# Graph convolutions by slots on one NeuronCore: 13 slots per pair, six gathered chunks per tile, blocks of nine tiles, tables kept in SBUF

## The chip, the cores and the metric

The kernel runs on one NeuronCore of a Trainium2 chip. The time is the device time of one execution in microseconds (us). The time before is the median of three runs. Beside these there is one profiled execution, from which all views, lines and durations come; it took longer than the unprofiled runs, and both are given below. The engines are PE (TensorE), DVE (VectorE), ACT (ScalarE), POOL (GpSimd) and SP (SyncE, which here issues the plain DMAs). Lines such as L1168 are lines of the kernel before.

## The reference

There are 12500 nodes with 128 features and 200000 edges, sorted by destination. Two layers with a residual are computed:

```python
h = relu(layernorm(x));  x = x + attention(h, edges, edge_attr)   # 8 heads, softmax over a node's incoming edges
h = relu(layernorm(x));  x = x + gcn(h)
# gcn: three times   h = conv(h, W, b);  relu after the first two;  h = batch_norm(h)
# conv: h = h @ W;  out[d] = sum over edges (s, d) and the loop (d, d) of h[s] * dinv[s] * dinv[d];  out + b
```

The widths are 128 -> 256 -> 128 -> 128. The norm dinv depends on a node's degree alone. The kernel scales the rows by dinv beforehand and the sums by dinv afterwards, so that a convolution is a plain sum of source rows for each destination.

## The kernel before

**Stages.** The prologue makes q, k and v. Attention runs over 106 tiles of TN = 118 destination nodes. Then place_edges (L681 to L817) sorts each tile's edges on DVE and writes tables. Then follow three convolutions, each with a dense transform behind it (L1211). The function fast (L661) holds all but the prologue. A second branch, conv_rows, is built in too, for edge lists that do not fit the slots; it does not run on this input.

**How a convolution sums.** The rows of the table are grouped by NS = 98 source blocks of 128 rows, all held in SBUF as hs. Each pair (tile, source block) has SB = 16 slots. An edge that finds a slot is served without a gather; what is left over goes to an overflow list of OV = 512 entries per tile, that is JO = 4 chunks of 128.

- `take(b)` (L1131) builds the slots of block b, TB = 8 tiles, so that 8 x 16 = 128 slots of one source block form a matrix. It loads the slot numbers gi (one byte each, the same for all partitions, L1136). DVE compares them with the partition number and so makes a selection matrix go (L1141), four source blocks at a time. PE multiplies it with hs (L1144), ACT copies the product from PSUM to stage (L1146), and after SG = 14 source blocks SP stores stage to m in DRAM (L1147). A block takes seven such groups, 98 products.
- `reduce(b)` (L1150) handles the 8 tiles of a block. For each tile POOL gathers the overflow rows from the table in DRAM (L1159, recorded at L150, the line of the helper gather), one indirect DMA per chunk. SP loads the tile's slots back from m as mr, 112 partitions of RC = 14 rows (L1162). DVE makes one-hot matrices oh from the destinations of slots (dsA, L1165) and of overflow (odA, L1166); both are recorded at L676, the line of one_hot. PE sums into zp: the tile's own rows tg (L1079), 14 products with mr (L1168) and 4 with the gathered rows (L1170).
- `finish` (L1070) is called for NG = 4 tiles at a time. It loads tg and the norms db, and after the products scales zp (L1082) and hands it on: to a product with W1 in the first convolution (L1241), else to a bias and ReLU on ACT; then come the statistics (L1185).

**What sets the order.** All loops are unrolled at build time. The kernel writes take(b) and then reduce(b - 2) (LEAD = 2, L1175). A scheduler orders each engine's instructions once, when the program is built, by the order in which they are written and by an estimate of when their inputs and buffers are free; on the chip each engine and each DMA queue then runs its list in order. Buffers: m 4 blocks, gi 2, go 3, stage 2, mr 3, rows 5 tiles, oh 2, and two PSUM banks each for gp, zp and hq.

**Tables.** place_edges stores four tables in DRAM: gi_d for take, ds_d for the slots' destinations, os_d and od_d for the overflow's sources and destinations. At its start, conv_slots loads dsA, osA and odA from them (L1119 to L1121), in runs of 56 or 16 bytes, in each of the three convolutions.

Of the kernel before, what the change touches and what calls it, by code (L numbers as in the profile page):

```python
# [37 lines left out]
SB = 16  # L38
OV = 512
JO = OV // P  # L40
TB = P // SB
SG = 14
RP = 112
# [5 lines left out]
def tile_gnn(ctx: ExitStack, tc: tile.TileContext, x, src, dst, ea, wqkvT, weT, w1, w2, w3, par, out):  # L49
# [20 lines left out]
    assert NS % SG == 0 and SL % RP == 0 and SL <= WE and NS * P * P < LATE and TN < P  # L70
    RC = SL // RP
# [20 lines left out]

    gi_d = dram.tile([NBK, NS, TB, SB], U8, name="gi_d")
    ds_d = dram.tile([NTT, SL], FP, name="ds_d")
    os_d = dram.tile([NTT, OV], I32, name="os_d")
    od_d = dram.tile([NTT, OV], FP, name="od_d")
# [563 lines left out]
    def fast():  # L660
# [3 lines left out]
        slotted = fc.tile([1, 1], I32, name="slotted")  # L664
        pars = fc.tile([P, 12], FP, name="pars")
# [13 lines left out]
        def place_edges(rt, ps):  # L679
# [8 lines left out]
            turn = 0  # L688

# [69 lines left out]
            xo = rt.tile([NTT, 2, OV], I32, name="xo")  # L759
            yo = rt.tile([NTT, OV], FP, name="yo")  # L760
            nc.vector.tensor_scalar(x[:, :OV], x[:, :OV], -1.0, None, op0=ALU.add)
            nc.vector.tensor_copy(xo[:, 0], x[:, :OV])
            nc.vector.tensor_scalar(xo[:, 1], xo[:, 0], P - 1, None, op0=ALU.bitwise_and)
            nc.vector.tensor_copy(yo, xo[:, 1])
            nc.sync.dma_start(od_d, yo)
            nc.vector.tensor_scalar(y[:, :OV], x[:, :OV], 0.0, None, op0=ALU.max)
            nc.vector.tensor_copy(xo[:, 0], y[:, :OV])
            nc.vector.tensor_scalar(xo[:, 0], xo[:, 0], 7, None, op0=ALU.logical_shift_right)
            nc.sync.dma_start(os_d, xo[:, 0])
# [35 lines left out]
            nc.sync.dma_start(ds_d, A[turn][:, :SL])  # L805
# [3 lines left out]
            for b in range(NBK):  # L809
                tn = min(TB, NTT - b * TB)  # L810
                nc.sync.dma_start(gi_d[b, :, :tn, :].rearrange("s t k -> t s k"),
                                  sl[b * TB:b * TB + tn, :].rearrange("t (s k) -> t s k", k=SB))
            if NTT % TB:
                none = rt.tile([NS, (TB - NTT % TB) * SB], U8, name="none")
                nc.vector.memset(none, 255)
                nc.sync.dma_start(gi_d[NBK - 1, :, NTT % TB:, :].rearrange("s t k -> s (t k)"), none)
# [252 lines left out]
        NST = -(-NTT // NG)  # L1069

        def finish(wk, table, t0, n, zp, use, ps, add):

            tg = wk.tile([TN, NG, D], FP, name="tg")
            nc.sync.dma_start(tg[:, :n, :], rows118(table, t0, n))
            db = wk.tile([P, NG * TN], FP, name="db")
            nc.sync.dma_start(db[:, :n * TN],
                              dinv_d[t0 * TN:(t0 + n) * TN].unsqueeze(0).to_broadcast([P, n * TN]))
            for i in range(n):
                nc.tensor.matmul(zp[:, i, :], tg[:, i, :], ident[:TN, :TN], start=True, stop=False)  # L1079
                add(i)  # L1080
            zt = wk.tile([P, NG * TN], FP, name="zt")
            nc.vector.tensor_tensor(zt[:, :n * TN], zp[:, :n].rearrange("p a b -> p (a b)"), db[:, :n * TN],  # L1082
                                    op=ALU.mult)
            use(wk, t0, n, zt[:, :n * TN], ps)

        def conv_rows(table, use):

            with ExitStack() as s:
                ew = s.enter_context(tc.tile_pool(name="ew", bufs=1))
                srcA = ew.tile([P, NTT, JJ], I32, name="srcA")  # L1090
                dlA = ew.tile([P, NTT, JJ], BF, name="dlA")
                nc.sync.dma_start(srcA, sw_d.rearrange("t (p j) -> p t j", j=JJ))
                nc.sync.dma_start(dlA, dlb_d.rearrange("t (p j) -> p t j", j=JJ))
                ga = s.enter_context(tc.tile_pool(name="ga", bufs=3))
                wk = s.enter_context(tc.tile_pool(name="wk", bufs=2))
                ps = s.enter_context(tc.tile_pool(name="ps", bufs=2, space=PSUM))
                for t0, n in groups(NTT, NG):
                    zp = ps.tile([P, NG, TN], FP, name="zp")

                    def add(i):  # L1100
                        rows = ga.tile([P, JJ, D], FP, name="rows")
                        for j in range(JJ):
                            gather(rows[:, j, :], table, srcA[:, t0 + i, j:j + 1])
                        oh = wk.tile([P, JJ, TN], FP, name="oh")
                        one_hot(oh, dlA[:, t0 + i, :])
                        for j in range(JJ):
                            nc.tensor.matmul(zp[:, i, :], rows[:, j, :], oh[:, j, :], start=False, stop=(j == JJ - 1))

                    finish(wk, table, t0, n, zp, use, ps, add)

        def conv_slots(table, use):


            with ExitStack() as s:
                tb = s.enter_context(tc.tile_pool(name="tb", bufs=1))
                dsA = tb.tile([RP, NTT, RC], FP, name="dsA")
                osA = tb.tile([P, NTT, JO], I32, name="osA")
                odA = tb.tile([P, NTT, JO], FP, name="odA")
                nc.sync.dma_start(dsA, ds_d.rearrange("t (p c) -> p t c", c=RC))  # L1119
                nc.sync.dma_start(osA, os_d.rearrange("t (p c) -> p t c", c=JO))  # L1120
                nc.sync.dma_start(odA, od_d.rearrange("t (p c) -> p t c", c=JO))  # L1121
                blocks = s.enter_context(tc.tile_pool(name="blocks", bufs=4, space=DRAM))
                gy = s.enter_context(tc.tile_pool(name="gy", bufs=2))
# [5 lines left out]
                ps = s.enter_context(tc.tile_pool(name="ps", bufs=2, space=PSUM))  # L1129

                def take(b):  # L1131
                    m = blocks.tile([TB * SB, NS, D], FP, name="m")
                    for s0 in range(0, NS, SG):
                        stage = sg.tile([P, SG, D], FP, name="stage")
                        gi = gy.tile([P, SG, P], U8, name="gi")
                        nc.sync.dma_start(gi.rearrange("p s m -> p (s m)"),  # L1136
                                          gi_d[b, s0:s0 + SG].rearrange("s t k -> (s t k)").unsqueeze(0)
                                          .to_broadcast([P, SG * P]))
                        for a, n in groups(SG, 4):
                            go = gx.tile([P, 4, P], FP, name="go")  # L1140
                            nc.vector.tensor_scalar(go[:, :n], gi[:, a:a + n], iota_q, None, op0=ALU.is_equal)  # L1141
                            gp = ps.tile([P, 4, D], FP, name="gp")
                            for i in range(n):
                                nc.tensor.matmul(gp[:, i, :], go[:, i, :], hs[:, s0 + a + i, :], start=True,  # L1144
                                                 stop=True)
                            nc.scalar.copy(stage[:, a:a + n, :], gp[:, :n, :])  # L1146
                        nc.sync.dma_start(m[:, s0:s0 + SG, :], stage)  # L1147
                    return m

                def reduce(b, m):  # L1150
                    for t0 in range(b * TB, min(NTT, (b + 1) * TB), NG):
                        n = min(NG, NTT - t0)
                        zp = ps.tile([P, NG, TN], FP, name="zp")

                        def add(i):
                            t = t0 + i
                            rows = ga.tile([P, JO, D], FP, name="rows")
                            for j in range(JO):
                                gather(rows[:, j, :], table, osA[:, t, j:j + 1])  # L1159
                            k = (t - b * TB) * SB  # L1160
                            mr = mt.tile([RP, RC, D], FP, name="mr")
                            nc.sync.dma_start(mr, m[k:k + SB].rearrange("k s d -> (k s) d")  # L1162
                                              .rearrange("(p c) d -> p c d", c=RC))
                            oh = wk.tile([P, RC + JO, TN], FP, name="oh")
                            one_hot(oh[:RP, :RC, :], dsA[:, t, :])  # L1165
                            one_hot(oh[:, RC:, :], odA[:, t, :])  # L1166
                            for j in range(RC):
                                nc.tensor.matmul(zp[:, i, :], mr[:, j, :], oh[:RP, j, :], start=False, stop=False)  # L1168
# [4 lines left out]
                        finish(wk, table, t0, n, zp, use, ps, add)  # L1173

                LEAD = 2  # L1175
                taken = []
                for b in range(NBK + LEAD):
                    if b < NBK:
                        taken.append(take(b))
                    if b >= LEAD:  # L1180
                        reduce(b - LEAD, taken[b - LEAD])

        def stats(st, h, t0, n):
            w = min(n * TN, N - t0 * TN)
            nc.vector.bn_stats(st[:, t0 // NG, :], h[:, :w])  # L1185
# [44 lines left out]
        def convolutions(conv):  # L1230
            with ExitStack() as s:
# [4 lines left out]
                def use1(wk, t0, n, zt, ps):  # L1236
                    a, b = t0 * TN, (t0 + n) * TN
                    hx = wk.tile([P, NG * TN], FP, name="hx")
                    for k, h in enumerate((big[:, a:b], hx[:, :b - a])):
                        hq = ps.tile([P, NG * TN], FP, name="hq")  # L1240
# [119 lines left out]
```

## Time and profile before

| | |
|---|---|
| median of 3 runs | 6388.98 us (6387.02 to 6391.8) |
| profiled execution, own time | 6587.43 us |
| its span, first to last instruction | 6585.6 us |
| busy: PE, DVE, POOL, ACT | 71%, 55%, 56%, 16% |
| DMA | 1134.9 MB in all; queue of SP 43.6% and of POOL 19.0% of 16 engines' span |
| HBM read, written | 797 MB, 332 MB |
| first to last gather of attention | 149 to 2801 us |
| first to last product of the convolutions | 3323.2 to 4369.4, 4461.5 to 5457.9, 5533.6 to 6525.9 us |

The page of the profile has the busy tenths of each engine in 40 equal slices of the span, with the granted clock of PE (PEclk) and the share of the DMA engines in use. Its groups are read so: line, engine, operation, what is written and read (partitions x elements), count | busy us, mean ns of one | idle us of the engine just before them, and what ended most of it. In the timeline a row gives start and length in us, engine, line and operation, how many instructions are merged, and in brackets the idle time before it with what ended it. SPq is the issue of a DMA by SP. PEld, the weight load, runs beside PE.

### The profile page before, as it was taken

The numbers are of one execution on the slowest core, as the hardware profiler recorded it, in microseconds if no ns is written. First come the engines' busy times: TensorE is split into PE (matmuls) and PEld (weight loads), VectorE is DVE, ScalarE is ACT, GpSimd is POOL, SyncE is SP. The second block draws the span as 40 slices with busy tenths as digits, with TensorE's granted clock in tenths as the row PEclk, the third lists the DMA queues.
The fourth block names the chain that finished last, engine by engine and source line by source line (L and its number), as shares of the span: only waits on it lengthen the run. The fifth ranks groups of instructions, "written<-read, shape, count | busy, mean of one in ns | idle before, by whom it ended". The sixth has DMA issues, their size and how long they took to land. (4 is left out here: it accounts for less than half of the span.)

```text
span 6585.6 us, 84666 instructions
## 1 busy us (share of the span) xinstructions
PE 4653.7 (71%) x30954; PEld 4338.3 (66%) x30954; DVE 3616.5 (55%) x6389; ACT 1073.6 (16%) x2501; POOL 3713.3 (56%) x2981
## 2 busy tenths in 40 slices
PE   5576776676666667710068888877888886888887
PEld 2566666666666666600068878877888886888887
DVE  7455655566565666699534444453444444444445
ACT  3111111111111111100022222202221212221220
POOL 1677777777777777700025555543556662556654
PEclk9677776777776777755588999998899998999988
DMA  6455555454454455400388888878788887888877
GB/s 181 131 134 130 137 133 131 127 126 127 117 128 124 124 132 129 112 5 3 42 211 238 232 243 243 234 191 225 242 244 246 246 233 183 245 249 240 241 230 205
DMA packets 710647, 1134.91 MB, mean 172 GB/s; under 512 B 299663, under 2 KB 528207, under 8 KB 710119
## 3 DMA queue, kind: packets, MB, share of 16 engines
q1 hardware_dynamic: 587581, 821.13, 43.6%
q0 software_dynamic: 122256, 306.67, 19.0%
q8 instruction: 251, 4.11, 0.3%
q10 hardware_dynamic: 388, 1.60, 0.1%
q14 instruction: 171, 1.40, 0.1%
HBM read 797.28 MB, written 331.80 MB: 171 GB/s over the span
## 5 line engine op out<-in xcount | busy, mean ns | idle before, releaser
L150 POOL DMA_INDIRECT rows<-t_d,osA x1272 | 1687.6, 1327 | 2034.8 <-PE zp L1079 773.6
L150 POOL DMA_INDIRECT kv<-kv_d,srcA x1696 | 2021.4, 1192 | 635.2 <-issue 491.7
L1144 PE MATMUL gp<-hs,go 128*128 128x128 f32 x8232 | 1134.8, 297 | 563.9 <-DMA rows<-t_d,osA 235.1
L1144 PEld LDWEIGHTS gp<-hs,go 128*128 128x128 f32 x8232 | 1060.7, 207 | 615.8 <-issue 480.5
L1168 PE MATMUL zp<-oh,mr 112*128 112x118 f32 x8904 | 1174.4, 290 | 133.6 <-DMA mr<-m 115.5
L1168 PEld LDWEIGHTS zp<-oh,mr 112*128 112x128 f32 x8904 | 1129.0, 206 | 148.5 <-issue 74.1
L945 PE MATMUL qe<-qt,oht 128*128 128x128 f32 x3392 | 869.1, 417 | 455.4 <-issue 192.6
L945 PEld LDWEIGHTS qe<-qt,oht 128*128 128x128 f32 x3392 | 775.0, 310 | 522.2 <-issue 368.2
L1141 DVE TENSOR_SCALAR go<-gi,iota_q 128x512 f32<-128x512 uint8 (+1 forms) x1176 | 512.8, 455 | 906.0 <-PE gp L1144 489.6
L676 DVE TENSOR_TENSOR oh<-iota_f,dsA 112x1652 f32<-112x1652 f32 x318 | 598.9, 1884 | 689.7 <-PE zp L1170 331.6
L1146 ACT COPY stage<-gp 128x512 f32<-128x512 f32 (+1 forms) x1176 | 599.4, 534 | 1736.5 <-PE gp L1144 1348.2
L946 DVE TENSOR_TENSOR kv<-qe,kv 128x512 f32<-128x512 f32 x424 | 289.0, 683 | 840.4 <-DMA kv<-kv_d,srcA 677.1
L1011 PE MATMUL acc<-vals,oh 128*118 128x137 f32 x3392 | 526.0, 323 | 110.5 <-DVE vals L1005 73.4
L1011 PEld LDWEIGHTS acc<-vals,oh 128*118 128x118 f32 x3392 | 504.9, 219 | 132.3 <-DVE vals L1005 91.3
L1170 PE MATMUL zp<-oh,rows 128*128 128x118 f32 x2544 | 343.7, 277 | 16.4 <-DMA rows<-t_d,osA 14.7
L1170 PEld LDWEIGHTS zp<-oh,rows 128*128 128x128 f32 x2544 | 314.8, 193 | 20.0 <-DMA rows<-t_d,osA 17.5
L1005 DVE TENSOR_TENSOR vals<-kv,vals 128x2048 f32<-128x2048 f32 x106 | 242.3, 2286 | 34.6 <-ACT vals L1004 13.1
L676 DVE TENSOR_TENSOR oh<-iota_f,dlA 128x1888 f32<-128x1888 f32 x106 | 224.4, 2117 | 61.4 <-remote 58.0
L961 PE MATMUL sm<-wbd,et 128*128 128x32 f32 x848 | 172.5, 362 | 115.6 <-DVE mg L998 92.4
L961 PEld LDWEIGHTS sm<-wbd,et 128*128 128x128 f32 x848 | 166.6, 292 | 124.8 <-DVE mg L998 99.5
L949 DVE TENSOR_REDUCE sc<-kv 128x128 f32<-128x2048 f32 x106 | 240.5, 2269 | 0.0
L676 DVE TENSOR_TENSOR oh<-iota_f,odA 128x472 f32<-128x472 f32 x318 | 203.6, 641 | 11.4 <-DMA odA<-od_d 11.4
(235 smaller groups left out, 3490.2 us busy)
## 6 DMA issues: line engine op xcount, KB each, us to landing
m<-stage SPq DMA_DIRECT2D x294, 896.0 KB
mr<-m SPq DMA_DIRECT2D x318, 784.0 KB
gi<-gi_d SPq DMA_DIRECT2D x294, 224.0 KB
dw_b<-dlb_d SPq DMA_DIRECT2D x106, 512.0 KB
kv<-kv_d,srcA POOLq DMA_INDIRECT x1696
ebx<-in_edge_attr_dram SPq DMA_DIRECT2D x106, 256.0 KB
rows<-t_d,osA POOLq DMA_INDIRECT x1272
tg<-t_d SPq DMA_DIRECT2D x78, 236.0 KB
```

The lines of the kernel that those rows point to most:

```text
L150: nc.gpsimd.indirect_dma_start(out=o, out_offset=None, in_=table[:, :], in_offset=bass.IndirectOffsetOnAxis(ap=idx, axis=0))
L676: nc.vector.tensor_tensor(oh, iota_f[:sh[0], :TN].unsqueeze(1).to_broadcast(sh), dl.unsqueeze(2).to_broadcast(sh), op=ALU.is_equal)
L945: nc.tensor.matmul(qe[:, k, :], ohv[:, :, j + k], qt, start=True, stop=True)
L946: nc.vector.tensor_tensor(qk[:, j:j + 4, :], qe, qk[:, j:j + 4, :], op=ALU.mult)
L961: nc.tensor.matmul(bias[:, 4 * k:4 * k + 4, :].rearrange("p j h -> p (j h)"), et[:, k, :], wbd, start=True, stop=True)
L1005: nc.vector.tensor_tensor(vh[:, :, :, :C], kv[:, :, D:].rearrange("p j (h c) -> p j h c", h=H), vh[:, :, :, C:].to_broadcast([P, JJ, H, C] ...
L1011: nc.tensor.matmul(acc, oh[:, j, :], va[:, j, :], start=(j == 0), stop=(j == JJ - 1))
L1141: nc.vector.tensor_scalar(go[:, :n], gi[:, a:a + n], iota_q, None, op0=ALU.is_equal)
L1144: nc.tensor.matmul(gp[:, i, :], go[:, i, :], hs[:, s0 + a + i, :], start=True, stop=True)
L1146: nc.scalar.copy(stage[:, a:a + n, :], gp[:, :n, :])
L1168: nc.tensor.matmul(zp[:, i, :], mr[:, j, :], oh[:RP, j, :], start=False, stop=False)
L1170: nc.tensor.matmul(zp[:, i, :], rows[:, j, :], oh[:, RC + j, :], start=False, stop=(j == JO - 1))
```

## The change

1. Slots and overflow: SB goes from 16 to 13, OV from 512 to 768, so that a tile has 1274 slots and six gathered chunks. A block has TB = 9 tiles (117 slots of a source block), and there are 12 blocks for 14.
2. A tile's slots are loaded as 127 partitions of RC = 10 rows and one of 4, in three DMAs; m is stored as 112 and 5 partitions, tg loaded as 112 and 6. gi has the tile outside and the slot inside, and go reads it permuted.
3. The order: one block is taken while the one before is reduced, and the tiles of the latter are written between the groups of the former. finish becomes a generator that yields after each tile. Groups of finish have GN = 3 tiles.
4. The tables dlS (destinations, bfloat16) and srcO (overflow's sources) stay in SBUF; the new helper turned fills them, with PE transposes. ds_d, os_d and od_d and their loads are gone. gi_d is stored in runs of 182 bytes.
5. The one-hot matrices of a tile are made by one instruction, from numbers that lie in PSUM (nums) and from dlS.

```diff
-SB = 16
-OV = 512
+SB = 13
+OV = 768
+GN = 3
...
+    RC = -(-SL // P)
+    LP, LR = divmod(SL, RC)
...
+        dlS = fc.tile([P, NTT, RC + JO], BF, name="dlS")
+        srcO = fc.tile([P, NTT, JO], I32, name="srcO")
...
+            def turned(a, n, o, copy):
+                av = a[:, :n * P].rearrange("t (p c) -> t c p", c=n)
+                for c, m in groups(n, 4):
+                    tp = ps.tile([P, 4, P], FP, name="et_p")
+                    for i in range(m):
+                        nc.tensor.transpose(tp[:, i, :NTT], av[:, c + i, :], ident[:NTT, :NTT])
+                    copy(o[:, :, c:c + m].rearrange("p t c -> p c t"), tp[:, :m, :NTT])
...
-            nc.sync.dma_start(od_d, yo)
+            turned(x1, JO, dlS[:, :, RC:], nc.scalar.copy)
...
-            nc.sync.dma_start(os_d, xo[:, 0])
+            turned(y1, JO, srcO, nc.vector.tensor_copy)
...
-            nc.sync.dma_start(ds_d, A[turn][:, :SL])
+            turned(A[turn], RC, dlS[:, :, :RC], nc.scalar.copy)
...
-                nc.sync.dma_start(gi_d[b, :, :tn, :].rearrange("s t k -> t s k"),
-                                  sl[b * TB:b * TB + tn, :].rearrange("t (s k) -> t s k", k=SB))
+                nc.sync.dma_start(gi_d[b, :, :tn, :].rearrange("g t k -> t g k"),
+                                  sl[b * TB:b * TB + tn, :].rearrange("t (g k) -> t g k", g=NS // SG))
...
-            nc.sync.dma_start(tg[:, :n, :], rows118(table, t0, n))
+            for a, b in ((0, 112), (112, TN)):
+                nc.sync.dma_start(tg[a:b, :n, :], rows118(table, t0, n, a, b))
...
                 nc.tensor.matmul(zp[:, i, :], tg[:, i, :], ident[:TN, :TN], start=True, stop=False)
                 add(i)
+                yield
...
-                nc.sync.dma_start(dsA, ds_d.rearrange("t (p c) -> p t c", c=RC))
-                nc.sync.dma_start(osA, os_d.rearrange("t (p c) -> p t c", c=JO))
-                nc.sync.dma_start(odA, od_d.rearrange("t (p c) -> p t c", c=JO))
-                blocks = s.enter_context(tc.tile_pool(name="blocks", bufs=4, space=DRAM))
-                gy = s.enter_context(tc.tile_pool(name="gy", bufs=2))
+                tb = s.enter_context(tc.tile_pool(name="tb", bufs=1, space=PSUM))
+                nums = tb.tile([P, TN], FP, name="nums")
+                nc.vector.tensor_copy(nums, iota_f[:, :TN])
+                blocks = s.enter_context(tc.tile_pool(name="blocks", bufs=3, space=DRAM))
+                gy = s.enter_context(tc.tile_pool(name="gy", bufs=3))
...
+                        gv = gi.rearrange("p t (s k) -> p s t k", k=SB)
                         for a, n in groups(SG, 4):
-                            nc.vector.tensor_scalar(go[:, :n], gi[:, a:a + n], iota_q, None, op0=ALU.is_equal)
+                            nc.vector.tensor_scalar(go[:, :n], gv[:, a:a + n], iota_q, None, op0=ALU.is_equal)
...
-                        nc.sync.dma_start(m[:, s0:s0 + SG, :], stage)
-                    return m
+                        for x, y in ((0, 112), (112, TS)):
+                            nc.sync.dma_start(m[x:y, g * SG:(g + 1) * SG, :], stage[x:y])
+                        yield
...
-                            nc.sync.dma_start(mr, m[k:k + SB].rearrange("k s d -> (k s) d")
-                                              .rearrange("(p c) d -> p c d", c=RC))
+                            for x, y, r in ((0, 112, RC), (112, LP, RC), (LP, LP + 1, LR)):
+                                nc.sync.dma_start(mr[x:y, :r], mv[x * RC:(y - 1) * RC + r]
+                                                  .rearrange("(p c) d -> p c d", c=r))
...
-                            one_hot(oh[:RP, :RC, :], dsA[:, t, :])
-                            one_hot(oh[:, RC:, :], odA[:, t, :])
+                            nc.vector.tensor_tensor(oh, nums.unsqueeze(1).to_broadcast(sh),
+                                                    dlS[:, t, :].unsqueeze(2).to_broadcast(sh), op=ALU.is_equal)
...
-                LEAD = 2
-                taken = []
-                for b in range(NBK + LEAD):
-                    if b < NBK:
-                        taken.append(take(b))
-                    if b >= LEAD:
-                        reduce(b - LEAD, taken[b - LEAD])
+                taken = None
+                for b in range(NBK + 1):
+                    tiles = reduce(b - 1, taken) if b else iter(())
+                    if b < NBK:
+                        taken = blocks.tile([TS, NS, D], FP, name="m")
+                        done = 0
+                        for g, _ in enumerate(take(b, taken)):
+                            while done < g * TB * SG // (NS - SG):
+                                next(tiles, None)
+                                done += 1
+                    for _ in tiles:
+                        pass
```

## The prediction

> **What bounds the kernel now.** I read the page first (slices, then groups), then one row per convolution from the busy times by stretch, then the timeline of a block and of the seams between convolutions. From the page, rows 2:
>
> ```profile
> POOL 1677777777777777700025555543556662556654
> PEclk9677776777776777755588999998899998999988
> DMA  6455555454454455400388888878788887888877
> ```
>
> Slices 1 to 17 (149 to 2801 us) are attention, 17 to 20 the placing of edges on DVE, 21 to 40 three convolutions. The change works on the last two only. The groups that matter there:
>
> ```profile
> L150 POOL DMA_INDIRECT rows<-t_d,osA x1272 | 1687.6, 1327 | 2034.8 <-PE zp L1079 773.6
> L1144 PE MATMUL gp<-hs,go 128*128 128x128 f32 x8232 | 1134.8, 297 | 563.9 <-DMA rows<-t_d,osA 235.1
> L1168 PE MATMUL zp<-oh,mr 112*128 112x118 f32 x8904 | 1174.4, 290 | 133.6 <-DMA mr<-m 115.5
> L1170 PE MATMUL zp<-oh,rows 128*128 128x118 f32 x2544 | 343.7, 277 | 16.4 <-DMA rows<-t_d,osA 14.7
> L676 DVE TENSOR_TENSOR oh<-iota_f,dsA 112x1652 f32<-112x1652 f32 x318 | 598.9, 1884 | 689.7 <-PE zp L1170 331.6
> ```
>
> Each product is two records: 8232 = 3 x 14 blocks x 98 slots x 2. By stretch, first to last product of each convolution:
>
> ```profile
> core 0: us, PE busy (x) PEld busy (x) DVE busy (x) ACT busy (x) POOL busy (x), PEclk, DMA share, GB/s
> 3323.20:4369.40 1046.20, 893.03 (x6880) 850.33 (x6880) 469.32 (x680) 233.56 (x446) 554.03 (x419) 0.92 0.80 235
> 4461.50:5457.90 996.40, 858.88 (x6768) 837.84 (x6768) 454.99 (x656) 216.66 (x418) 554.66 (x417) 0.91 0.80 239
> 5533.60:6525.90 992.30, 846.74 (x6712) 825.41 (x6712) 447.59 (x643) 213.10 (x410) 557.46 (x414) 0.92 0.79 237
> ```
>
> PE is the busiest at 86%, DMA is at 80%, and POOL waits for PE (773.6 us). The rest of PE's time is lost where a block turns from building slots to reducing and back:
>
> ```profile
> 4800.22 0.94 POOL L150 DMA_INDIRECT rows<-t_d,osA  x1 [0.30 <-issue]
> 4800.90 0.65 DVE L1082 TENSOR_TENSOR zt<-zp,db 128x472 f32<-128x472 f32 x1 [1.80 <-PE zp L1170]
> ...
> 4809.39 1.88 DVE L676 TENSOR_TENSOR oh<-iota_f,dsA 112x1652 f32<-112x1652 f32 x1 [1.03 <-PE zp L1170]
> 4809.48 3.16 POOL L150 DMA_INDIRECT rows<-t_d,osA  x1 [0.30 <-issue]
> 4811.19 0.64 DVE L676 TENSOR_TENSOR oh<-iota_f,odA 128x472 f32<-128x472 f32 x1
> 4812.76 4.98 PE L1168 MATMUL zp<-oh,mr 112*128 112x118 f32 x28 [3.19 <-DMA mr<-m]
> 4818.70 3.29 PE L1168 MATMUL zp<-oh,mr 112*128 112x118 f32 x28
> ```
>
> Two things to see. PE waits 3.19 us for a transfer and then does 14 products in 4.98 us that take 3.29 warm. And a gather takes 0.94 us beside a DVE operation that reads PSUM (zp), but 3.16 us when DVE builds a one-hot from two SBUF operands: it ends 0.8 us after DVE does. The seam before the second convolution:
>
> ```profile
> 4433.65 7.51 SPq L1120 DMA_DIRECT2D osA<-os_d  x1
> 4441.20 7.78 SPq L1121 DMA_DIRECT2D odA<-od_d  x1
> 4461.48 5.47 PE L1144 MATMUL gp<-hs,go 128*128 128x128 f32 x28 [28.50 <-issue]
> ```
>
> **The change, part by part**, per convolution (106 tiles) unless said.
>
> *PE.* Slot products 14 x 98 = 1372 become 12 x 98 = 1176; reduction products 14 per tile become 10, gathered ones 4 become 6. By the groups' busy time per product (1134.8/4116 = 0.276 us, 1174.4/4452 = 0.264, 343.7/1272 = 0.270) and 41 us for tg: before 378 + 391 + 115 + 41 = 925 (groups overlap a little in PE's 859), after 325 + 280 + 172 + 41 = 818. So 107 us less, if PE alone decided.
>
> *Bytes.* m 90 -> 84 x 117 x 7168 B = 70 MB; mr 85 -> 106 x 1274 x 512 B = 69; gi 22.5 -> 17.6; gathers 28 -> 42; tg and db 6.4 each. Together 238 -> 212 MB, or 885 us at the 239 GB/s of now.
>
> *POOL.* 424 gathers become 636. A gather alone takes 0.947 us (median), plus 0.305 between two. At today's mean of 1.327 that is 636 x 1.632 = 1038 us, more than a whole convolution now: everything hangs on the one-hot numbers in PSUM. The Trainium skill speaks against them (SBUF — State Buffer, Who interferes with whom): a DVE instruction with two SBUF inputs contends only with GpSimd's reads, and descriptor generation needs the write interface, "inferred". By that rule today's stretch has another cause and stays: 1038 us. The trace contradicts it (3.16 us under oh, 0.94 under zt), and the gathers of the convolutions beside which DVE does nothing last 0.946 us on average, 0.962 at most. So I take the trace: with one PSUM operand the stretch goes. What is left is go, which reads one SBUF tile: gathers that overlap go alone average 0.998 us in the second and third convolutions. I take 0.998 for all: 6 x 1.303 = 7.82 us per tile, 829 us in all; the ends are 796 (0.947) and 1038. POOL thus becomes the bound. A stage with POOL as its bound is at hand: attention has 1696 gathers, 2021.4 + 1696 x 0.305 = 2539 us of POOL's own in 2652 us, 95.7%. The same share gives 829/0.957 = 866 us, 8.17 per tile.
>
> *DVE.* One oh of 128x1888 for 1884 + 641 ns; the dlA form of L676 (same size) takes 2117, and a PSUM operand costs nothing (zt: 650 ns for 472 columns, the odA form 641). go works on 468 numbers in permuted order: 0.42 us, or 0.65 if it goes one by one like oh. DVE is 46% busy and stays under POOL at both ends: nothing.
>
> *SP.* m in two pieces, mr in three, tg in two: 356 issues become about 678, 322 x 0.32 us = 103 us of SP. SP waits 644 us for stage and 587 for zp in all: hidden; if not, 103. The skill's DMA: Bandwidth & Descriptors (Rules for kernel authors) says that splitting by partitions is pointless; its own rule on the number of engines (Why a DMA increments its semaphore by 16 and not by 1) gives one transfer of 118 partitions two engines and 112 sixteen. No view shows a packet's engine; by the first rule tg's split costs 36 issues (12 us of SP), by the second it removes some of the 115.5 us for mr. I count neither.
>
> *Order.* A tile's mr now waits for a block finished just before, not one block earlier, and in SP's queue gi loads and m stores stand behind it, PE's slot products behind those. Between the last slot group and that tile the written order puts two tiles and two groups, about 2 x 3.8 + 2 x 3.3 = 14 us of PE; a store took 6.1 us until stage was free again (3367.4 to 3373.5) and an mr 4.3 (4808.5 to 4812.8), 10.4 in all. Cost nothing; at most 8 us a boundary, 11 boundaries, and POOL's five buffered tiles cover most. That slot and reduction products alternate evens out the DMA load; I book no more than POOL's pace allows.
>
> *GN 3.* 36 finishes for 27, some 0.4 us of DVE each: hidden.
>
> *Placing edges (once).* SL falls from 1568 to 1274: 11 steps of 6.4 us and some 20 us of single passes, -17. OV grows: ten shifts x 0.53, one 0.4, masks 1.6, waits for 12 transposes 0 to 6: +11. DVE -6. The gi_d stores go from 784 runs of 16 B a block to 63 of 182 B: the issue of 34.3 us and its wait (41.5) becomes about 8, -33. Table loads of 20.3 + 10.0 + 7.8 us share the queues with hs; hs alone, 6.4 MB, needs 23 at 278 GB/s (the stretch from 3350 to 3400 us) of now 52, less a gi load: -26. The ten transposes of the slot table (three groups of 1.06 PE + 0.59 ACT, rows L954 and L957) run beside the gi_d stores: nothing, +5 uncovered. PE starts at 3323 - 65 = 3258.
>
> *Seams.* 28.5 and 32.3 us before the second and third convolutions become about 5, what a gi load needs.
>
> **Sum.** First: from 3258, slots of block 0 take 26 us and the first tile follows 13 later, 3297; five tiles are gathered by then; 101 x 8.17 + 5 = 830, end 4127 for 4369.4: -242. Second: transform 62 + start 5 + 866 + 5 = 938 for 1088.5: -150. Third: 43 + 876 = 919 for 1068: -149. Together -541. The profiled execution took 6587.4 (span 6585.6): 6046. The median of the runs shown is 0.970 of it (6388.98): **5865 us**.
>
> **Rivals.**
> 1. *POOL without losses* (829 us): 4092, 901, 882, -650: 5760. For it: 0.30 between gathers is steady. Against: attention's 4.3%. Chance 0.20.
> 2. *DMA is the bound at today's 239 GB/s* (885 us): -224, -131, -130 = -485: 5920. For it: slices at 8 and 9. Against: it can do more, 278 GB/s from 3350 to 3400 us, where slots are built alone. Chance 0.27.
> 3. *The gathers stay stretched* (slower; place: POOL under oh): 1038/0.957 = 1085 us: -34, +68, +70 = +104: 6490. It decides from 1049 us per convolution on, a mean gather of 1.27 us. For it: the skill's rule, and oh stays 2.1 us per tile; against: zt's neighbours. 0.05.
> 4. *PE cools*: waiting for each tile, it gets attention's clock of 0.70 for 0.92: 818 x 0.92/0.70 = 1075, 6460. The skill (TensorE: Matmul & The Clock Gate, HAM oscillation) halves the clock after idle windows of 3.4 us; here waits would be 1 to 2 us, and after 0.5 us the trace stays warm. 0.03.
>
> The forecast (POOL at 95.7%) has 0.45. Under 0.2% (13 us) a change cannot be told from none here. Slower: rivals 3 and 4 with most of their chance, 0.06; same 0.02; faster 0.92. The range goes from below rival 1 (gathers at 0.947: another -90) to DMA at 220 GB/s (962 us, 6140), less the outer ends: 5680 to 6080.
>
> **What would show it.** Right: gathers at a mean of 0.95 to 1.0 us; POOL busy plus 0.3 per gather over 90% of a convolution; PE waiting for rows; seams under 8 us; PE's clock at 0.85 or more. Wrong: gathers above 1.27 us; POOL waiting for PE with DMA at 0.9 (rival 2); long PE waits for mr at each block's first tile (the order).

## The result, and the profile after

The kernel after takes 6323.43 us (median of 4 runs, 6313.77 to 6331.95), the kernel before 6388.0 (4 runs): a ratio of 0.990, 95% interval 0.988 to 0.992. It is faster by 1.0%, against a forecast of 5865 us (8.2% faster). Lines are now those of the kernel after: L148 the gathers, L1157 and L1159 the slot products and ACT's copies, L1161 the stores of stage, L1178 the loads of mr, L1186 and L1188 the products with mr and with gathered rows.

The rows of the page that stood first in the prediction, now:

```profile
POOL 0777777777777777710335656535666664666663
PEclk9677776777767777755588888898889888888988
DMA  6655555555455454400178888877888887888888
```

POOL has hardly filled up (5 to 6 tenths in the convolutions, where about 7 were forecast), and PE's clock has fallen from 9 to 8 tenths. The groups on the page:

```profile
L148 POOL DMA_INDIRECT rows<-t_d,srcO x1908 | 1849.0, 969 | 1683.0 <-issue 492.2
...
L1182 DVE TENSOR_TENSOR oh<-nums,dlS 128x1888 f32<-128x1888 f32 x318 | 674.3, 2121 | 1514.9 <-PE zp L1188 1514.6
L1186 PE MATMUL zp<-oh,mr 128*128 128x118 f32 x6360 | 967.9, 319 | 563.9 <-DMA mr<-m 437.0
...
L1157 PE MATMUL gp<-hs,go 128*117 128x128 f32 x7056 | 892.3, 281 | 111.3 <-DVE go L1154 68.7
```

The gathers have lost their stretch: 969 ns for 1327. In its place PE waits 563.9 us ahead of the products with mr; the same column had 133.6 before. One row per convolution, from the first slot product to the last product with gathered rows, with the columns of the prediction's third view (length, busy time of PE, PEld, DVE, ACT and POOL, clock, DMA share, GB/s):

```profile
3174.10:4189.00 1014.90, 804.44 (x6096) 775.49 (x6096) 402.34 (x545) 211.18 (x406) 579.18 (x606) 0.88 0.81 214
4251.60:5231.60 980.00, 770.79 (x5951) 752.22 (x5952) 382.47 (x509) 191.12 (x371) 608.88 (x635) 0.88 0.84 216
5273.80:6253.50 979.70, 768.84 (x5952) 750.75 (x5952) 382.18 (x509) 191.25 (x371) 609.27 (x635) 0.89 0.85 217
```

PE's work fell from 859 to 771 us in the second convolution, yet that convolution is only 16 us shorter. The timeline shows where it went. The tile that waits here is the middle one of its group of three (rows of SP's queue, ACT and PE, the others left out):

```profile
4571.64 0.31 SPq L1178 DMA_DIRECT2D mr<-m  x1
...
4579.81 0.68 SPq L1161 DMA_DIRECT2D m<-stage  x2
...
4580.54 0.78 SPq L1178 DMA_DIRECT2D mr<-m  x1
...
4585.70 0.87 ACT L1159 COPY stage<-gp 117x512 f32<-117x512 f32 x2 [0.39 <-PE gp L1157]
...
4586.00 0.38 PE L1092 MATMUL zp<-ident,tg 118*128 118x118 f32 x2
...
4586.60 0.67 SPq L1161 DMA_DIRECT2D m<-stage  x2
4587.31 2.94 SPq L1178 DMA_DIRECT2D mr<-m  x4
...
4591.39 4.12 PE L1186 MATMUL zp<-oh,mr 128*128 128x118 f32 x20 [5.01 <-DMA mr<-m]
```

Read it by SP's rows. A tile's mr is three transfers. The first goes out at 4571.64, the second at 4580.54, the third only at 4587.31, the last two each behind a pair of stores of stage. A store can't go before ACT has copied (to 4586.57), and ACT can't before PE has made the slot products. PE then turns to the tile itself (4586.00), and has to wait for one partition of four rows that was not yet asked for. The transfer lands 4 us later. The program's own list for SP has just this order (here from the first convolution). It comes back, mostly with two or three pairs of stores, for the middle tile in 33 of each convolution's 36 groups:

```
mr 112 partitions
m<-stage 112, m<-stage 5
hb_d<-hx
mr 15
m<-stage 112, m<-stage 5
mr 1
```

There are 102 gaps of over 1.5 us ahead of products with mr, most of them 4.8 to 7 us, 562 us in all; 95 are at the middle tile of a group. For 23 of them, 116 us, the trace names no releaser; they stand in the same place as the others and go with the same edits below. The products after a gap run slower: 4.12 us for 20 records here, 2.40 for the tile at 4571.98 that did not wait.

**A caution on the two profiles.** The profiled execution of the kernel after took 6313.77 us, like its unprofiled runs; that of the kernel before took 198 us more than its median. Attention, whose code is the same, ends 85 us later there (2798 against 2713). One trait goes with it: in attention PE waits longer for nothing that the trace shows. These are the rows of that wait (us in all, times, longest) in the kernel before and in the kernel after:

```profile
PE qe L945 <- issue: 192.6, 100, 7.9
PE qe L957 <- issue: 82.2, 37, 6.2
```

All nine profiles of the kernel after and its variants on the faster chips (told apart in the experiments) have 82 to 95 us in this row, all nine profiles on the slower ones 179 to 217. So the profile on which the forecast rests has the trait of the slower chips, though the median beside it does not; what it comes from is open. The sums of the two profiles therefore don't make up the 65 us between the medians, and stages are compared between them with this in mind.

Placing the edges, from attention's last gather to the first product, shrank by 64 us (525 to 461). That is steady: in the other profiles it takes 516 to 522 us with the tables of the kernel before and 461 or 462 with those of the kernel after. It is about the whole gain. From the first slot product to the last product of the third convolution the two profiles have 3203 and 3079 us. If the 113 us of the long profile that attention doesn't explain lie there, which isn't shown, the convolutions with their seams gained some 10 us net.

### The profile page after: what moved, and what is told of

The parts are those of the page before. It is cut to its first block, busy times and chain, and to the rows that moved or that the text cites. A ratio compares the mean times of both kernels' runs of the same rounds, so it can differ in the third digit from the quotient of the medians.

```text
span 6312.0 us, 80526 instructions
## 1 busy us (share of the span) xinstructions
PE 4409.4 (70%) x28564; PEld 4112.4 (65%) x28564; DVE 3403.5 (54%) x5972; ACT 1008.0 (16%) x2374; POOL 3874.7 (61%) x3617
## 5 line engine op out<-in xcount | busy, mean ns | idle before, releaser
L148 POOL DMA_INDIRECT rows<-t_d,srcO x1908 | 1849.0, 969 | 1683.0 <-issue 492.2
L148 POOL DMA_INDIRECT kv<-kv_d,srcA x1696 | 2021.4, 1192 | 549.5 <-issue 479.5
L1182 DVE TENSOR_TENSOR oh<-nums,dlS 128x1888 f32<-128x1888 f32 x318 | 674.3, 2121 | 1514.9 <-PE zp L1188 1514.6
L1186 PE MATMUL zp<-oh,mr 128*128 128x118 f32 x6360 | 967.9, 319 | 563.9 <-DMA mr<-m 437.0
L1186 PEld LDWEIGHTS zp<-oh,mr 128*128 128x128 f32 x6360 | 926.4, 233 | 582.9 <-DMA mr<-m 327.3
L1157 PE MATMUL gp<-hs,go 128*117 128x128 f32 x7056 | 892.3, 281 | 111.3 <-DVE go L1154 68.7
L1157 PEld LDWEIGHTS gp<-hs,go 128*117 128x117 f32 x7056 | 832.4, 184 | 150.6 <-issue 102.9
L1159 ACT COPY stage<-gp 117x512 f32<-117x512 f32 x1008 | 521.7, 532 | 1363.4 <-PE gp L1157 855.6
L1154 DVE TENSOR_SCALAR go<-gi,iota_q 128x468 f32<-128x468 uint8 x1008 | 426.7, 455 | 221.4 <-DMA gi<-gi_d 111.2
L1188 PE MATMUL zp<-oh,rows 128*128 128x118 f32 x3816 | 511.2, 287 | 0.0
L1188 PEld LDWEIGHTS zp<-oh,rows 128*128 128x128 f32 x3816 | 490.7, 206 | 0.0
```

The costliest lines, as they stand in the source:

```text
L148: nc.gpsimd.indirect_dma_start(out=o, out_offset=None, in_=table[:, :], in_offset=bass.IndirectOffsetOnAxis(ap=idx, axis=0))
L1154: nc.vector.tensor_scalar(go[:, :n], gv[:, a:a + n], iota_q, None, op0=ALU.is_equal)
L1157: nc.tensor.matmul(gp[:, i, :], go[:, i].rearrange("p t k -> p (t k)"), hs[:, g * SG + a + i, :], start=True, stop=True)
L1182: nc.vector.tensor_tensor(oh, nums.unsqueeze(1).to_broadcast(sh), dlS[:, t, :].unsqueeze(2).to_broadcast(sh), op=ALU.is_equal)
L1186: nc.tensor.matmul(zp[:, i, :], mr[:q, j, :], oh[:q, j, :], start=False, stop=False)
L1188: nc.tensor.matmul(zp[:, i, :], rows[:, j, :], oh[:, RC + j, :], start=False, stop=(j == JO - 1))
```

## Experiments

Ratios are to the kernel before, run beside on the same chip. The chips differ: on two of five occasions it took 6352 to 6354 us, on three 6628 to 6765, and those three stand apart at the end. Each chip was used on one occasion, so a chip and an occasion can't be told apart here.

Theories: **Q**, the order in SP's list keeps the last pieces of mr behind stores; **D**, the DMA engines are full; **S**, transfers of 15 and 1 partitions land late by themselves; **B**, too few buffers for mr.

### The kernel after again

> The kernel after, unchanged, on one chip with the next two, since the first four experiments ran on a chip on which the kernel before took 6765 us for 6388, and the kernel after was not among them. If the ratio of 0.990 belongs to the kernel, it comes again within 0.5%. If it belongs to the chip, that is, if the kernel after suffers more from what makes that chip slow, then on a chip with a slow kernel before the ratio lies at 1.03 to 1.05, where its two variants lay.

6303.7 us, ratio 0.991 (0.989 to 0.993). The result repeats.

### The stores on ACT

```diff
-                            nc.sync.dma_start(m[x:y, g * SG:(g + 1) * SG, :], stage[x:y])
+                            nc.scalar.dma_start(m[x:y, g * SG:(g + 1) * SG, :], stage[x:y])
```

> The kernel after with the stores of stage issued by ACT, once more, now beside the kernel after. Theory Q (SP's queue): on a chip where the kernel before takes about 6390 us it takes about 5990 us, 5% below the kernel after; PE's waits for mr fall below 120 us in all. Theory D (the DMA engines are full): within 0.5% of the kernel after. On a slow chip Q expects it 1 to 3% below the kernel after, with waits for mr as small, and the rest of PE's idle time without a releaser.

5787.33 us, ratio 0.910 (0.908 to 0.913), 8.2% below the kernel after; this is called the mended kernel below. The convolutions, and the two groups that matter:

```profile
3165.70:3985.10 819.40, 752.17 (x6096) 716.72 (x6096) 400.31 (x544) 207.80 (x406) 582.79 (x606) 0.96 0.91 265
4048.90:4868.00 819.10, 718.94 (x5952) 701.68 (x5952) 387.95 (x509) 185.53 (x371) 606.90 (x635) 0.95 0.92 258
4911.30:5730.30 819.00, 718.78 (x5952) 699.57 (x5952) 387.03 (x509) 186.27 (x371) 609.82 (x635) 0.95 0.93 259
```

```profile
L148 POOL DMA_INDIRECT rows<-t_d,srcO x1908 | 1851.0, 970 | 1169.5 <-issue 482.6
...
L1186 PE MATMUL zp<-oh,mr 128*128 128x118 f32 x6360 | 809.1, 281 | 74.7 <-DMA mr<-m 73.2
```

No transfer, no byte and no buffer changed, only the queue that the stores stand in. PE's idle time ahead of these products falls from 564 to 75 us, its clock rises to 0.95, and the core moves 259 GB/s for 216. D falls, and S with it: the small pieces are still there. The gain is larger than the 5% that Q expected. One thing did move along: the scheduler also orders PE's list anew, and only 76 of the 318 tiles still come after the same number of slot products as in the kernel after. By itself this experiment can't exclude that the new order did it; the next one can. All three convolutions take 819 us, and POOL needs 636 x (0.970 + 0.303) = 810 of them: it has become the bound.

### One transfer per tile

```diff
-                            for x, y, r in ((0, 112, RC), (112, LP, RC), (LP, LP + 1, LR)):
-                                nc.sync.dma_start(mr[x:y, :r], mv[x * RC:(y - 1) * RC + r]
-                                                  .rearrange("(p c) d -> p c d", c=r))
+                            mo = m[k:k + SB + 1].rearrange("k s d -> (k s) d")
+                            nc.sync.dma_start(mr, mo[:P * RC].rearrange("(p c) d -> p c d", c=RC))
...
-                        taken = blocks.tile([TS, NS, D], FP, name="m")
+                        taken = blocks.tile([TS + 1, NS, D], FP, name="m")
+                        nc.sync.dma_start(taken[TS, :P * RC - SL, :], ident[:P * RC - SL, :])
```

> The kernel after with a tile's mr as one transfer, once more, now beside the kernel after. Theory Q: 2 to 4% below the kernel after on a chip where the kernel before takes about 6390 us; the waits for mr fall by a third or more. Theory S (transfers of 15 and 1 partitions land late by themselves): 5% below, and more than with the stores on ACT. Theory D: within 1% of the kernel after.

5816.78 us, ratio 0.914 (0.913 to 0.916), 7.7% below the kernel after; idle time ahead of the products 72.8 us. Here the stores stay in SP's queue, and 256 of the 318 tiles keep their place among PE's slot products. Of the 102 tiles that PE had to wait for, 72 keep it, and ahead of these its idle time falls from 359 to 10 us. So it is the loads that were late, and not the order of PE's list that made PE wait.

It is more than the 2 to 4% that Q said: loads of mr still stand behind stores in SP's list, but PE finds only 13 of them over 1.5 us late, 11 in the first convolution. S had expected 5% or more here, and less from the stores on ACT, which gained 8.2%. So it was less the stores by themselves than a tile whose pieces lie apart on both sides of them. Either edit is enough.

### Both

> The kernel after with both edits: stores of stage issued by ACT and a tile's mr as one transfer. Theory Q: no store stands before a load and nothing is left behind, so it equals the stores on ACT alone within 1%, about 5980 us where the kernel before takes 6390, with POOL as the bound: its busy time plus 0.3 us for each of 636 gathers over 90% of a convolution of 870 us.

5791.32 us, ratio 0.911 (0.909 to 0.913), as with the stores on ACT alone. The second convolution here, to be set beside the middle row above:

```profile
4039.00:4858.60 819.60, 726.68 (x5952) 702.82 (x5952) 389.70 (x509) 188.28 (x371) 609.40 (x635) 0.95 0.83 258
```

The share of the DMA engines is 0.83 for 0.92, at the same rate and the same length of the stage. A share of 0.92 was no bound.

### More buffers

```diff
-                mt = s.enter_context(tc.tile_pool(name="mt", bufs=3))
+                mt = s.enter_context(tc.tile_pool(name="mt", bufs=5))
```

> The kernel after with five buffers for mr instead of three, once more, beside the kernel after. Theory B (buffers): 5 to 8% below the kernel after. Theory Q (SP's queue): within 1% of the kernel after, since in SP's list the stores still stand between the pieces of every third tile; waits for mr above 400 us.

6302.26 us, ratio 0.991 (0.989 to 0.994); the kernel after beside it 6297.13. The waits stay (PE's, on the whole program):

```profile
PE zp L1186 <- DMA mr<-m: 432.1, 78, 7.9
```

B falls. In SP's list two or three pairs of stores still stand between the first and the last pieces of every third tile.

> The kernel after, unchanged, beside these. On a chip where the kernel before takes about 6390 us: ratio 0.990 again. On a slow chip: above 1, at 1.03 to 1.08, since its two mended variants lay at 1.04 there and a wait for mr is added.

That run of the kernel after: ratio 0.990 (0.988 to 0.993).

### The numbers in SBUF, in the mended kernel

```diff
-                            nc.vector.tensor_tensor(oh, nums.unsqueeze(1).to_broadcast(sh),
+                            nc.vector.tensor_tensor(oh, iota_f[:, :TN].unsqueeze(1).to_broadcast(sh),
```

This on top of the stores on ACT.

> The stores on ACT and the one-hot matrices from the numbers in SBUF, once more. If POOL bounds the mended kernel: mean gather 1.20 to 1.23 us, POOL 636 x (1.215 + 0.30) = 964 us per convolution for 819, ratio to the kernel before 0.975 to 0.985 on a chip where the stores on ACT give 0.910. If not, 0.910.

6219.67 us, ratio 0.978 (0.976 to 0.981), as expected. The page, the second convolution, and what PE waits for in it:

```profile
L148 POOL DMA_INDIRECT rows<-t_d,srcO x1908 | 2280.4, 1195 | 1180.0 <-issue 496.5
```

```profile
4190.50:5149.50 959.00, 781.61 (x5951) 747.11 (x5952) 388.35 (x509) 189.05 (x371) 748.04 (x635) 0.90 0.80 220
```

```profile
PE zp L1188 <- DMA rows<-t_d,srcO: 141.9, 126, 3.3
```

Gathers of 1.195 us make 636 x 1.498 = 953 us of POOL's own, and the convolution takes 959; with 0.970 it was 810 and 819. The stage follows POOL one to one, and the place of one operand of DVE is worth 140 us per convolution.

### Transfers undivided

Both edits, and tg as one transfer of 118 partitions, a store as one of 117.

> Stores on ACT, mr, tg and stores undivided, once more. If a transfer of 118 partitions runs on two engines only: 0.5 to 2% above the kernel with divided tg and stores (ratio 0.911), with waits for tg. If the count does not matter: within 0.3% of 0.911.

5807.63 us, ratio 0.914 (0.911 to 0.916) against 0.911 (0.909 to 0.913) on another occasion: the intervals overlap, and the time shows neither theory. The packets show more. Those of tg are the ones of 512 bytes in SP's queue. In the second convolution, the packets for three tiles take 6.5 us from the first to the last and at most 4 are under way at once; with the divided tg of the kernel with both edits it is 2.8 us and 13 at once (medians of 33 groups). So the undivided transfer is slower, as the first theory said; its engines themselves are not in the trace. But PE hardly waits for it:

```profile
PE zp L1091 <- DMA tg<-t_d: 11.5, 3, 5.6
```

### On the slower chips

On the first of the three the kernel before took 6765 us. The expectations are for the kernel before, profiled again; then, each as the only edit of the kernel after, the stores on ACT, one transfer of mr, and the numbers in SBUF:

> The kernel before, unchanged, profiled a second time, since its first profiled execution took 198 us longer than its median. If that execution was long in attention, attention's last gather comes about 85 us earlier than 2798 us (the kernel after has it at 2713), and the rest of the 198 us must be missing from the three convolutions, which then take about 1010, 960 and 955 us instead of 1046, 996 and 992. If it was long elsewhere, attention's last gather stays near 2798 us and the convolutions keep their lengths.

> The kernel after with one edit: ACT issues the stores of stage to m, right after its own copies, and SP keeps only loads. The transfers and their number stay. Theory Q (SP's queue): PE's waits of 5 to 8 us at every third tile come from pieces of mr that stand behind a store of stage in SP's list, and that store waits for the slot products which PE makes just before the tile. Then the waits for mr (437 us, and 116 more without a releaser) fall below 120 us, POOL's 636 gathers become the bound, a convolution takes about 870 us for 980, and the time is about 5990 us, a ratio to the kernel before of 0.94. Theory D (the DMA engines are full at a share of 0.84): the transfers land as late as before, the waits stay above 400 us, the time stays within 0.5% of 6323.

> The kernel after with one edit: a tile's mr is one transfer of 128 partitions by 10 rows instead of three of 112, 15 and 1 partitions (six rows that no product reads come from the next tile's slots or a padding row); stores stay with SP. 636 transfers fewer. Theory Q: no piece of a tile can be left behind alone, but one whole mr in three still stands between two stores in SP's list; the waits fall by a third to two thirds, time 6080 to 6200 us. Theory S (the small transfers of 15 and 1 partitions are what lands late, by their few engines): all waits go here and none with the stores on ACT: about 5990 us. Theory D: within 1% of 6323, since the bytes stay.

> The kernel after with one edit: the one-hot matrices are made from the numbers in SBUF, not from their copy in PSUM. The forecast had the gathers stretched in that case. A tile has one matrix of 2.12 us, and a gather beside such an operation ended 0.8 us after it in the kernel before: mean gather 1.15 to 1.33 us for 0.97, POOL 636 x (1.15 to 1.33 + 0.30) = 922 to 1037 us for a convolution that now takes 980: time 6320 to 6500 us. If the operand's place does not matter, the mean gather stays at 0.97 us and the time within 0.3% of 6323.

The second profile of the kernel before has attention's last gather at 2954 us and convolutions of 1049, 1034 and 1047 us, so it doesn't settle where the first one's 198 us lay. Stores on ACT: ratio 1.038 (1.033 to 1.044). One mr: 1.041 (1.035 to 1.046). Numbers in SBUF: 1.050 (1.044 to 1.057), mean gather 1.228 us. No time came as expected, but the mean gather did, and PE's waits for mr did what Q said: 40 us with the stores on ACT, 81 with one transfer, 373 where the queue was left as it was.

On the second it took 6628 us. Five buffers; numbers in SBUF with the stores on ACT; transfers undivided; and the kernel before with its stores on ACT:

> The kernel after with five buffers for mr instead of three; three transfers per tile, stores with SP. Theory B (buffers: a tile's load is late because its buffer comes free late): PE's waits for mr mostly go, ratio to the kernel before 0.91 to 0.93, as with the stores on ACT. Theory Q (SP's queue): in SP's list the first piece of every third tile still has two or three pairs of stores between it and the last pieces, so the waits stay above 400 us and the ratio is 0.99.

> The kernel after with the stores on ACT (5787 us, ratio 0.910) and the one-hot matrices made from the numbers in SBUF. The gathers then last 1.23 us on average, as they did with the numbers in SBUF alone, for 0.97, and POOL takes 636 x (1.23 + 0.30) = 973 us per convolution. Since POOL is now the bound at 819 us per convolution, this costs about 150 us in each: time 6240 us, ratio 0.98. If POOL is not the bound, the ratio stays within 0.5% of 0.910.

> The kernel after with the stores on ACT, mr as one transfer (5791 us, ratio 0.911), and now tg as one transfer of 118 partitions and a store of stage as one of 117. If a transfer of 118 partitions runs on two engines only, tg lands several us later, PE waits for tg at the start of each group of three tiles, and the ratio rises by 0.5 to 2%. If the partition count does not matter, the ratio stays within 0.3% of 0.911.

```diff
-                        nc.sync.dma_start(m[:, s0:s0 + SG, :], stage)
+                        nc.scalar.dma_start(m[:, s0:s0 + SG, :], stage)
```

> The kernel before with one edit: ACT issues its stores of stage. It tells how much of the gain of the stores on ACT was there to be had without the change. In the second convolution of the kernel before, PE waits 38.9 us for mr and 33.7 us for ACT's copies into stage. Theory Q: these 73 us in each convolution mostly go, ratio 0.97 to 0.98. If the kernel before is bound by PE and the DMA engines alone, within 0.5% of 1.

Ratios: five buffers 1.115 (1.111 to 1.120), numbers in SBUF with stores on ACT 0.997 (0.994 to 0.999), undivided 1.024 (1.020 to 1.027), the kernel before with the stores on ACT 0.986 (0.980 to 0.992).

> The kernel before with its stores of stage issued by ACT, once more. If its waits for mr and for ACT's copies (38.9 and 33.7 us in the second convolution) mostly go: ratio 0.97 to 0.985. If the block order that it is written in keeps PE from using the earlier loads: within 0.5% of 1.

The same edit on the third (6647 us): 0.984 (0.979 to 0.989). So moving the stores alone gives the kernel before some 1.5% there; no such run fell on a faster chip. PE's waits for ACT's copies fell, from 97 and 110 us in the two profiles of the kernel before to 56 and 60. Those for mr did not go as expected: 154 and 143 us, for 116 and 126. The change with its stores moved gains 9% on the faster ones.

What these chips do is not explained. The undivided kernel took 6780 us on one of them and 5808 on a faster chip. This row is first among PE's waits on the slower one, and absent on the other:

```profile
PE gp L1156 <- issue: 527.2, 189, 9.2
```

"issue" means that PE waits for nothing that the trace shows. Against the faster chips the kernel before loses 4 to 6.5% there, the undivided one 17%, the one with stores on ACT 21%. Every verdict above rests on the faster chips. The unmended kernel after was not run there, so on which side of 1 it lies is open; with five buffers, which takes the same time as it on the faster chip, it was 1.115.

## Why the prediction was wrong, step by step

**The step that failed** is *Order*, with *SP*. It asked whether a tile's block is stored in time, found 14 us of cover, and wrote "Cost nothing; at most 8 us a boundary, 11 boundaries". The block was stored in time: among SP's waits there is no load of mr that waited for a store to land. What was late was the request for a tile's last pieces, and in the middle of a group of three tiles rather than at a block's first tile: 102 waits, 562 us in all. *SP* priced the extra issues by their own length (103 us, "hidden, if not 103") and *Order* named the gi loads and m stores in SP's queue, but neither asked for which piece PE waits while the store ahead of it waits for PE's previous work. SP did stand waiting for ACT's copies, 469 us of the second convolution, which the sum took for spare time. The profile of before gave no plain sign. Its mr stood ahead of 115.5 us of idle PE, and its stores waited for ACT in the same queue, but moving those stores did not shorten its waits for mr (on the slower chips).

**Splitting.** The Trainium skill, DMA: Bandwidth & Descriptors (Rules for kernel authors), holds splitting by partitions pointless. I counted it at nothing; here the split of mr cost 487 us (6304 to 5817), by the queue and not by the transfers, since with the stores on ACT the same pieces cost nothing (5787). The other rule weighed there, on partitions and engines, fits the packets of the undivided tg, at most 4 at once for 13; in the time it makes no difference that can be told from none.

**Gathers and PSUM**: right. Forecast 0.998 us a gather, measured 0.969; with SBUF numbers 1.195, where 1.327 was the cautious end. The skill's rule in SBUF — State Buffer (Who interferes with whom), with its inferred remark that descriptor generation needs the write interface, would have left them stretched; the trace decided rightly against it. The runs don't tell whether the remark is wrong or whether a gather, which takes its row numbers from SBUF (srcO), counts as a read.

**POOL as the bound**: right for the mended kernel, 810 of 819 us (99%) for a forecast of 95.7% of 866. Rival 1 (829 us, without losses) came nearest. In the kernel after it is not reached: 810 of 980.

**PE**: the forecast's 107 us less is 88 in the kernel after and 140 in the mended one; the rest is its clock, 0.88 for 0.91, then 0.95. Rival 4 (PE cools) had the right sign and the wrong wait: 1 to 2 us were expected, most were 4.8 to 7. The page cited there (TensorE: Matmul & The Clock Gate, HAM oscillation) agrees with 4.12 us for 20 records after a 5 us gap, 2.40 without. But the mean clock stayed at 0.88: in the second convolution the trace has 36 stretches at half clock, 227 of 980 us in all (86 of 819 in the mended kernel).

**Bytes**: 212 MB forecast; 216 GB/s x 980 us = 212. **Rival 2** (DMA at 239 GB/s) is refuted: 259 GB/s in the mended kernel.

**Placing edges** -65 forecast, -64 measured; only the sum was measured, not its parts. **Seams** about 5 us forecast, 4.9 and 5.2 measured. **DVE**: oh 2.12 us, go 0.455 for 0.42.

**The sum.** The forecast had 866 us per convolution; it takes 1015, 980 and 980, 377 us more (2975 - 3 x 866). That is the mis-sized term. Two others cancel in part. I took 0.970 of the whole sum for the long profile, which took off 181 us, though the 866 us came from POOL's own durations and did not need it; and attention, the same code, ended 85 us earlier than I had it. 377 - 85 + 181 = 473, for a miss of 458. The mended kernel's 5787 us lies inside the range and only 78 below the forecast. That nearness is in part luck: its convolutions are 140 us shorter than forecast in all (3 x 866 - 2457) and its attention is shorter too, and the 181 us taken off hide most of that.

## What to carry to other kernels

Ask of every queue not how long its issues take but what stands ahead of the piece that the bound engine needs next: a load behind a store that waits for that same engine's previous work cost 5 to 7 us each time here, the transfer included, though the queue looked idle. Try to issue a store from the engine that makes its data (worth 8.2% in the kernel after, some 1.5% in the kernel before), and do not divide a load whose pieces the scheduler may set apart. Where one engine's operation is stretched by another's operands, price it by the durations that overlap in the trace.

## What the runs showed of the hardware

The packets of 5120 bytes of mr took 314 ns on average with mr as 112, 15 and 1 partitions and 227 ns as 128 (second convolution, stores on ACT), at the same rate in all; the share of busy DMA engines fell from 0.92 to 0.83 and the time stayed. The packets of a transfer of 118 partitions took 6.5 us with at most 4 at once, of 112 and 6 partitions 2.8 us with 13.

A gather beside a DVE operation with two SBUF operands is stretched, beside the same operation with one of them in PSUM it is not. In the mended kernel, gathers that overlap the making of oh last 0.955 us on average with the numbers in PSUM and 1.80 us with them in SBUF; gathers with no DVE operation beside them last 0.943 and 0.945.

And the same kernels took 4 to 21% longer on some chips than on others.
